# A planned eight-layer kernel: rotary rows swapped by DMA, and one group's keys and values made early

## The chip, the cores and the metric

The kernel runs on one NeuronCore of a Trainium2 chip. The metric is device time in microseconds (us) for one execution of the whole program. A core has five engines, each with its own instruction queue: TensorE (PE, matmuls, with PEld for its weight loads), VectorE (DVE), ScalarE (ACT), GpSimd (POOL) and SyncE (SP, which here only issues DMAs). Each engine takes its instructions in the order in which they stand.

## The reference

`x` is 64 sequences of 64 tokens with 128 features, `ctx` a context of the same size. Four layers follow each other, each with an attention and an FFN branch, gated and added to `x` after a layernorm:

```python
x = x + jnp.tanh(g_xattn[0]) * _L0_xattn_ref(_layernorm(x), ctx, ctx, ...)   # mLSTM
x = x + jnp.tanh(g_ffn[0]) * _L0_ffn_ref(_layernorm(x), ...)                 # mixture-of-experts attention
x = x + jnp.tanh(g_xattn[1]) * _L1_xattn_ref(_layernorm(x), ctx, lens, ...)  # 16 heads of 64, RMS-normed q and k
x = x + jnp.tanh(g_ffn[1]) * _L1_ffn_ref(_layernorm(x), ...)                 # one adapter of 8 per sequence
x = x + jnp.tanh(g_xattn[2]) * _L2_xattn_ref(_layernorm(x), ctx, ...)        # 16 heads of 8, rotary q and k
x = x + jnp.tanh(g_ffn[2]) * _L2_ffn_ref(_layernorm(x), ...)                 # top 2 of 8 experts of 176, one shared
x = x + jnp.tanh(g_xattn[3]) * _L3_xattn_ref(ctx, ctx, _layernorm(x), mask, ...)
x = x + jnp.tanh(g_ffn[3]) * _L3_ffn_ref(_layernorm(x), ...)                 # fake-quantised, one scale over all of x
```

Three of them matter here. In layer 1's attention the keys are `rms_norm(ctx @ Wk)` and the values `ctx @ Wv`: neither needs `x`. In layer 2's attention each head's features are rotated in pairs:

```python
xe, xo = x[..., ::2], x[..., 1::2]
re, ro = xe * cos - xo * sin, xe * sin + xo * cos
```

In layer 1's FFN every token gets `b_base` and its expert's `ba_up`.

## The kernel before

The 4096 tokens are 8 groups of 512 (4 tiles of 128). A unit of work is one layer of one group: a pair (n, g), where n from 0 to 7 counts the eight branches above. `ORDER` lists the 64 pairs; `program` walks it and lets each branch's function record its instructions. Nothing is issued then. `Plan` keeps each operation with what it depends on, and `Plan.order` afterwards puts them into queues: a list scheduler with a price per operation (`cost`), eight PSUM banks and a number of SBUF slots per size (`SLOTS`, 42 of 2 KB). An operation's rank is its place in the recording. An operation that opens a slot and depends on no other slot's content (a load, a memset) is tied to an earlier operation of its stream, so that it does not come too early; `behind` and `plan.after` add such ties by hand. While `plan.after` is set, each DMA that is recorded waits for that operation. Where the planner foresees PE idle for long enough it puts in filler matmuls of `ident` with itself (`keep_clock`; they carry line 2074), to keep TensorE's clock granted. On each engine the order so made is the order in which the chip runs.

The weights of branch n+1 are loaded on ACT's queue when the first group of branch n has been recorded (`weights[n + 1]`), with `plan.after` set to that group's first operation `begun[n]`; for the first branch this is done after its second group, and the two 2 MB expert tables `ve` and `oe` wait besides for marks in that group's gates.

The parts that the change touches:

- `l0_xattn`, the first branch: the gate values of a group go to DRAM and back twice (`gd`, `rd`) before the attention matmuls (L1021, L1029, L1045). `l0_ffn` has PE's largest groups, the value experts (L1208) and the output experts (L1263), which read the one-hot rows `ohd` by DMA (L1254); its values are moved to other partitions by SBUF-to-SBUF DMAs (L1224).
- `l1_xattn`: for a tile, `project` makes queries and keys (L1322 to L1333), then come the values (L1350), the transposes (L822, in `transpose4`) and their copies (L1364, L1366), and the scores.
- `l1_ffn`: the biases are added by a matmul of `pick`, the one-hot of the expert with a row of ones, with `W["bias"]` (L1557), both f32.
- `l2_xattn`: `rotated` makes the pair-swapped rows by a second matmul with a weight whose columns are swapped (`wqs`, `wks`, L1706), and multiplies both from PSUM by `cos` and `sin` on DVE (L1708, L1712).
- `l2_ffn`: 1584 hidden rows in 12 chunks of 128 and one of 48, for gate (L1834) and up (L1835); its down weights `wd` are loaded in 29 pieces (L1758) from ACT.

Weights are loaded by `load` (L739), the context by `ctx_T` (L813).

Of the kernel before, what the change touches and what calls it, by code (L numbers as in the profile page):

```python
# [27 lines left out]
P = 128  # L28
# [16 lines left out]
    "b2k": (2048, 42),  # L45
# [26 lines left out]
class View:  # L72
# [40 lines left out]
    def region(self, exact=False):  # L113
# [8 lines left out]
        key = (row, c0, v.shape[1:], v.strides[1:])  # L122
        if key in View.bits:
            return p0, p0 + v.shape[0], View.bits[key]
# [7 lines left out]
        return p0, p0 + v.shape[0], View.bits[key]  # L132

    def real(self):
# [9 lines left out]
        ap = [[step, self.v.shape[0]]] + [[st, n] for n, st in zip(self.v.shape[1:], self.v.strides[1:])]  # L144
# [74 lines left out]
def cost(op):  # L219
# [12 lines left out]
    if meth == "indirect_dma_start":  # L232
        return 1300.0, 2000.0, None
# [59 lines left out]
class Plan:  # L293
    def __init__(self, tc, slots):
# [6 lines left out]
        self.hold, self.urgent = [], False  # L301
# [16 lines left out]
    def add(self, eng, meth, args, kw):  # L318
# [65 lines left out]
        if op.opens and op.opens[0].pool is not None:  # L384
# [424 lines left out]
def ctx_T(k, g):  # L809

    t = k.tile([P, GT], tag="cT")
    with k.behind(*k.begun):
        k.nc.sync.dma_start(out=t, in_=k.a["ctxT"][:, g * GT : (g + 1) * GT])  # L813
    return t
# [282 lines left out]
def l0_ffn_weights(k):  # L1097
    k.l0f = {n: k.load("l0f_" + n) for n in ("wgate", "wq", "wk")}

    for n, m in (("ve", k.marks[4]), ("oe", k.marks[5])):  # L1100
        k.plan.after = m
        k.l0f[n] = k.load("l0f_" + n)
# [171 lines left out]
def l1_xattn_weights(k):  # L1274
    k.l1x = {n: k.load("l1x_" + n) for n in ("wq", "wk", "wv", "qn", "kn")}
# [7 lines left out]
    k.l1x["lens"] = k.load("l1x_lens", dt=I32)  # L1283


def l1_xattn(k):
# [51 lines left out]
    def unit(g, t, xT, cT, past):  # L1338
        tok = slice(t * P, (t + 1) * P)
        tt = g * TG + t  # L1340

        nq = [project(xT[:, tok], W["wq"], half, None) for half in range(2)]
        nk = [project(cT[:, tok], W["wk"], half, valid[:, tt : tt + 1]) for half in range(2)]

        vt = [k.tile([P, C, DH], tag="vt") for _ in range(2)]
        for b in range(2):
            pv = k.ps()
            k.plan.wait(nq[1], nk[1])
# [8 lines left out]
            nc.scalar.copy(vt[b].rearrange("p c d -> p (c d)"), pv)  # L1357

        qT, kT = [], []
        for half in range(2):  # L1360
            qT.append(k.tile([P, 4, P], tag="qT"))
            kT.append(k.tile([P, 4, P], tag="kT"))
            pq = transpose4(k, nq[half])
            nc.scalar.copy(qT[half].rearrange("p c i -> p (c i)"), pq)  # L1364
            pk = transpose4(k, nk[half])
            nc.scalar.activation(kT[half].rearrange("p c i -> p (c i)"), pk, AF.Copy, scale=wqk)  # L1366
# [67 lines left out]
    def whole(g):  # L1434
        xT, cT = ln_T(k, g), ctx_T(k, g)
# [8 lines left out]
        for t in range(TG):  # L1444
            unit(g, t, xT, cT, past)
# [755 lines left out]
```

## Time and profile before

| | us |
|---|---|
| median of 4 runs | 1994.06 (1988.18 to 2003.24) |
| profiled execution | 1999.16 |
| its span, first to last instruction | 1997.4 |
| PE busy in it | 1896.3 |
| of that, filler matmuls (L2074, 806 records) | 113.7 |
| DVE, ACT, POOL busy | 1358.5, 1031.5, 1012.2 |
| mean granted TensorE clock | 0.974 of full |

A row of the groups reads: line, engine, operation, output tile <- input tiles, shapes, count of records, busy time in us, mean of one in ns, idle time of the engine before them and what ended it. An f32 matmul stands in it as two records, a transpose or a bf16 matmul as one. Stretches are given in us from the span's start. In the chain of waits a piece is a start, a length and what ran. In the trace `b2k`, `b1k` and the like are SBUF slots by size, `ps` a PSUM bank.

### The profile page before, as it was taken

To read this page: it belongs to the slowest core of one execution; us is meant where nothing else is said; L and a number is where in the kernel's file an instruction comes from. 1 tells how busy PE (TensorE), PEld (TensorE's weight loads), DVE (VectorE), ACT (ScalarE), POOL (GpSimd) and SP (SyncE) were. 2 spreads that over 40 slices of the span, in tenths; PEclk is the share of its full clock that TensorE was granted. 3 is DMA by queue.
4 is the path that set the end of the run, shared out by engine and by line. 5 is a ranking of instruction groups with operands and counts; after the bars stand their busy time and mean duration, and the time that the engine had idled before them with its cause. 6 is when DMAs were issued, how large, how long until landed. Compare 5 with 4: busy or idle time off the path is not lost.

```text
span 1997.4 us, 45509 instructions
## 1 busy us (share of the span) xinstructions
PE 1896.3 (95%) x17127; PEld 1133.8 (57%) x17127; DVE 1358.5 (68%) x3172; ACT 1031.5 (52%) x2896; POOL 1012.2 (51%) x1656
## 2 busy tenths in 40 slices
PE   8999999989999999999999999999999999999997
PEld 6654457545545466746554466644555457774575
DVE  2667775767886577678775568676887376775468
ACT  5452277534445568835242577641436377444465
POOL 5621475424526667546214786433246774444745
PEclk8799999999999989999999999999999999999999
DMA  4223300142123200011133200014211400102311
GB/s 149 94 56 89 105 2 14 28 125 75 44 88 86 79 12 12 24 54 58 51 86 99 66 16 13 22 43 137 56 62 45 114 2 2 57 20 66 93 59 43
DMA packets 117836, 117.19 MB, mean 59 GB/s; under 512 B 56371, under 2 KB 76903, under 8 KB 117359
## 3 DMA queue, kind: packets, MB, share of 16 engines
q1 hardware_dynamic: 106680, 97.71, 17.7%
q10 hardware_dynamic: 7863, 10.23, 1.6%
q0 software_dynamic: 3072, 6.33, 1.1%
q8 instruction: 135, 2.21, 0.4%
q14 instruction: 86, 0.70, 0.1%
HBM read 98.53 MB, written 8.09 MB: 53 GB/s over the span
## 4 chain that ended last, share of the span: by engine, by line
PE 71%; DVE 10%; POOL 6%; DMA 4%; ACT 3%; issue 3%; SPq 1%; another core or an unknown queue 0%; ACTq 0%; DVEq 0%; POOLq 0%
PE ps L1208 10%; PE ps L1263 8%; PE ps L822 8%; PE ps L1840 4%; PE ps L1835 4%; PE ps L1834 4%; POOL b L760 4%; PE ps L1637 3%; PE ps L1428 3%; PE ps L2074 3%; PE ps L1322 3%; PE ps L1350 2%; PE ps L1415 2%; PE ps L1235 1%; PE ps L1599 1%
## 5 line engine op out<-in xcount | busy, mean ns | idle before, releaser
L760 POOL TENSOR_TENSOR b<-b,neghalf 128x8 f32<-128x8 f32 (+1 forms) x208 | 304.5, 1464 | 17.2
L1208 PE MATMUL ps<-w_l0f_ve,b2k 128*128 128x512 f32 x512 | 244.9, 617 | 11.5 <-DVE b2k L1432 5.7
L759 POOL TENSOR_SCALAR b<-b 128x8 f32<-128x8 f32 (+1 forms) x208 | 42.9, 206 | 379.9 <-DVE b L788 254.4
L1263 PE MATMUL ps<-b2k,w_l0f_oe 128*128 128x512 f32 x512 | 230.2, 598 | 5.0 <-DVE b2k L1261 5.0
L1214 DVE COPY_PREDICATED b2k<-b1k,ps 128x512 f32<-128x512 int32 x224 | 162.5, 726 | 64.6 <-PE ps L1208 41.8
L1261 DVE TENSOR_TENSOR b2k<-b2k,b2k 128x512 f32<-128x512 f32 x256 | 171.5, 723 | 31.1 <-DMA b2k<-ohd 13.1
L1081 DVE TENSOR_REDUCE b<-ps 128x8 f32<-128x512 f32 x224 | 146.0, 681 | 58.1 <-PE ps L1386 24.2
L1839 POOL TENSOR_TENSOR b2k<-b2k,b2k 128x512 f32<-128x512 f32 (+1 forms) x104 | 131.6, 1288 | 96.6 <-DMA b2k<-cwd 43.5
L1263 PEld LDWEIGHTS ps<-b2k,w_l0f_oe 128*128 128x128 f32 x512 | 94.8, 191 | 121.7 <-issue 83.0
L1208 PEld LDWEIGHTS ps<-w_l0f_ve,b2k 128*128 128x128 f32 x512 | 94.4, 196 | 111.4 <-issue 78.7
L1082 DVE TENSOR_TENSOR b4k<-ps,b 128x512 f32<-128x512 f32 x224 | 148.3, 677 | 8.0 <-PE ps L822 7.7
L822 PE MATMUL ps<-ident,b2k 128*128 128x128 f32 x896 | 132.5, 278 | 7.6 <-DVE b2k L1333 3.2
L822 PEld LDWEIGHTS ps<-ident,b2k 128*128 128x128 f32 x896 | 102.7, 141 | 63.1 <-issue 32.2
L822 PE MATMUL ps<-ident,b4k 128*128 128x128 f32 x896 | 129.4, 281 | 7.1 <-ACT b4k L1625 5.5
L1838 DVE TENSOR_TENSOR b2k<-b2k,ps 128x512 f32<-128x512 f32 (+1 forms) x104 | 70.6, 684 | 93.0 <-PE ps L1835 74.1
L1084 ACT ACTIVATE b4k<-b4k 128x64 f32<-128x64 f32 x512 | 125.4, 251 | 14.9 <-DVE b4k L1082 13.6
L822 PEld LDWEIGHTS ps<-ident,b4k 128*128 128x128 f32 x896 | 102.9, 143 | 52.2 <-issue 25.8
L1837 ACT ACTIVATE b2k<-ps 128x512 f32<-128x512 f32 (+1 forms) x104 | 61.2, 596 | 137.7 <-PE ps L1834 107.2
L2074 PE MATMUL ps<-ident 128*128 128x128 f32 x806 | 113.7, 295 | 4.6 <-issue 2.2
L1333 DVE TENSOR_TENSOR b2k<-ps,b 128x512 f32<-128x512 f32 x128 | 87.4, 685 | 44.7 <-POOL b L1330 26.2
L1327 DVE TENSOR_REDUCE b<-b2k 128x8 f32<-128x512 f32 x128 | 84.2, 677 | 42.1 <-ACT b2k L1324 41.5
L2074 PEld LDWEIGHTS ps<-ident 128*128 128x128 f32 x806 | 104.7, 206 | 13.1 <-issue 7.7
(366 smaller groups left out, 4108.0 us busy)
## 6 DMA issues: line engine op xcount, KB each, us to landing
b2k<-ohd SPq DMA_DIRECT2D x256, 128.0 KB
b2k<-cwd SPq DMA_DIRECT2D x40, 256.0 KB
b2k<-in_ctxT SPq DMA_DIRECT2D x32, 256.0 KB
b2k<-b2k SPq DMA_DIRECT2D x128, 64.0 KB
b2k<-cwd SPq DMA_DIRECT2D x16, 224.0 KB
b2k<-cwd SPq DMA_DIRECT2D x16, 192.0 KB
b2k<-cwd SPq DMA_DIRECT2D x16, 160.0 KB
b2k<-cwd SPq DMA_DIRECT2D x24, 96.0 KB
```

Source lines behind the costliest of these rows:

```text
L760: k.nc.gpsimd.tensor_tensor(out, out, k.neghalf[:, :n], ALU.pow)
L822: k.nc.tensor.transpose(ps[:, t * P : (t + 1) * P], src[:, t, :], k.ident)
L1081: nc.vector.tensor_reduce(mx, src, AX.X, ALU.max)
L1082: nc.vector.tensor_tensor(out, src, bc(mx, 2, S), ALU.subtract)
L1084: nc.scalar.activation(out[:, n, :], out[:, n, :], AF.Exp, accum_out=den[n])
L1208: nc.tensor.matmul(pe, xT[:, t * P : (t + 1) * P], W["ve"][:, e * 512 : (e + 1) * 512], start=True, stop=True)
L1214: nc.vector.copy_predicated(acc, bc(ohi[:, t * H : (t + 1) * H, e], 2, DH), pe.rearrange("p (h d) -> p h d", d=DH))
L1261: nc.vector.tensor_tensor(so, oT[c], pick[:, u, :], ALU.mult)
L1263: nc.tensor.matmul(py, W["oe"][:, n * P : (n + 1) * P], so, start=(n == 0), stop=(n == C * E - 1))
L1333: nc.vector.tensor_tensor(n.rearrange("p c (r d) -> p (c r) d", r=2), ps.rearrange("p (h d) -> p h d", d=DH), bc(r, 2, DH), ALU.mult)
L1839: nc.gpsimd.tensor_tensor(h[:cn], h[:cn], cb[:cn], ALU.mult)
L2074: plan.spare = (sys._getframe().f_lineno, k.ident, k.ident.t.writes[-1][0])
```

## The change

- `l2_xattn`'s `rotated` has one matmul. ACT adds the bias and copies the result to SBUF; two DMAs on SP write the swapped rows (even partitions from odd ones and the other way round) into a second tile; three SBUF operations multiply and add. For the keys the last two of them run on POOL.
- In `l1_xattn` the group that `ORDER` names first for this branch is `eager`: its context load, keys and values are recorded ahead of its layernorm, and without ties, so that they can run as early as their operands land. `wk`, `wv`, `qn`, `kn` and `lens` of this branch are loaded with layer 0's FFN weights, ahead of `ve` and `oe`. That context load is then the unit's first operation, and so `begun[2]`, which the loads of `l1_ffn_weights` wait for.
- `l1_ffn`'s bias is split into three bf16 parts that stand 32 rows apart and are summed by the matmul; `pick` is bf16.
- `l2_ffn`'s last chunk has one matmul for gate and up, with a weight `last` of 112 columns. Its weights are loaded in turn: gate, then up after a third of the unit recorded last, then down after two thirds, down on SP instead of ACT.
- The planner has 45 slots of 2 KB and another price for an indirect DMA; regions know strided partitions. `ORDER` is another.

```diff
-    "b2k": (2048, 42),
+    "b2k": (2048, 45),
...
     if meth == "indirect_dma_start":
-        return 1300.0, 2000.0, None
+        return 1220.0, 1700.0, None
...
-        if op.opens and op.opens[0].pool is not None:
+        if op.opens and op.opens[0].pool is not None and not self.eager:
...
 def l0_ffn_weights(k):
     k.l0f = {n: k.load("l0f_" + n) for n in ("wgate", "wq", "wk")}
 
+    k.l1x = {n: k.load("l1x_" + n) for n in ("wk", "qn", "kn", "wv")}
+    k.l1x["lens"] = k.load("l1x_lens", dt=I32)
+
     for n, m in (("ve", k.marks[4]), ("oe", k.marks[5])):
...
 def l1_xattn_weights(k):
-    k.l1x = {n: k.load("l1x_" + n) for n in ("wq", "wk", "wv", "qn", "kn")}
+    k.l1x["wq"] = k.load("l1x_wq")
...
     def whole(g):
-        xT, cT = ln_T(k, g), ctx_T(k, g)
+        early = [None] * TG
+        eager = g in k.eager
+        if eager:
+            cT = ctx_T(k, g, True)
+            for t in range(TG):
+                kT = [turned(n, wqk) for n in keys(g, t, cT)]
+                early[t] = kT, values(t, cT, kT)
+        xT = ln_T(k, g)
+        if not eager:
+            cT = ctx_T(k, g)
...
-            unit(g, t, xT, cT, past)
+            unit(g, t, xT, cT, past, early[t])
...
-    bias = k.l1f["bias"] = k.fixed("w_l1f_bias", [P, D])
-    nc.gpsimd.memset(bias, 0.0)
-    nc.scalar.dma_start(out=bias[:64], in_=k.a["l1f_bias"])
+    parts = k.l1f["bias"] = k.fixed("w_l1f_bias", [P, D], BF16)
...
+    for r in range(3):
+        nc.sync.dma_start(out=rest[32 * r : 32 * r + 8], in_=k.a["l1f_bias"][:8])
+        nc.sync.dma_start(out=rest[32 * r + 8 : 32 * r + 9], in_=k.a["l1f_bias"][32:33])
+    for r in range(3):
+        rows = slice(32 * r, 32 * r + 32)
+        nc.vector.tensor_copy(part, rest)
+        nc.vector.tensor_copy(parts[rows], part[rows])
+        nc.vector.tensor_tensor(rest, rest, part, ALU.subtract)
...
-        pick = k.tile([P, NB, S], tag="pick")
-        nc.vector.tensor_scalar(pick, bc(owns, 2, S), k.ident[:, 32:33], None, ALU.add)
+        pick = k.tile([P, NB, S], BF16, tag="pick")
+        nc.vector.tensor_scalar(pick, bc(owns, 2, S), k.l1at[:, 8:9], None, ALU.add)
...
     def rotated(src, weight, bias, last):
 
-        out = []
-        for s, table in (("", "cos"), ("s", "sin")):
-            ps = k.ps()
-            nc.tensor.matmul(ps, W[weight + s], src, start=True, stop=True)
-            o = k.tile([P, NB, S], tag="rot" + s)
-            nc.vector.scalar_tensor_tensor(
-                o, ps.rearrange("p (b s) -> p b s", s=S), W[bias + s], bc(W[table], 1, NB), ALU.add, ALU.mult
+        ps = k.ps()
+        nc.tensor.matmul(ps, W[weight], src, start=True, stop=True)
+        y, ys = (k.tile([P, GT], tag="rot") for _ in range(2))
+        nc.scalar.activation(y, ps, AF.Identity, bias=W[bias])
+        for r in range(2):
+            nc.sync.dma_start(
+                out=ys.rearrange("(i r) n -> r i n", r=2)[r], in_=y.rearrange("(i r) n -> r i n", r=2)[1 - r]
             )
-            out.append(o)
-        last.tensor_tensor(out[0], out[0], out[1], ALU.add)
-        return out[0].rearrange("p b s -> p (b s)")
+        yv, ysv = (v.rearrange("p (b s) -> p b s", s=S) for v in (y, ys))
+        nc.vector.tensor_tensor(yv, yv, bc(W["cos"], 1, NB), ALU.mult)
+        last.tensor_tensor(ysv, ysv, bc(W["sin"], 1, NB), ALU.mult)
+        last.tensor_tensor(y, y, ys, ALU.add)
+        return y
...
 def l2_ffn_weights(k):
-    k.l2f = {n: k.load("l2f_" + n) for n in ("gate", "wg", "wu")}
+    k.l2f = {"gate": k.load("l2f_gate")}
+
+    last = k.l2f["last"] = k.fixed("w_l2f_last", [P, 112])
+    k.nc.gpsimd.memset(last, 0.0)
+    at, end = k.done
+    for n, name in enumerate(("wg", "wu")):
+        t = k.l2f[name] = k.fixed("w_l2f_" + name, [P, 1536])
+        k.nc.scalar.dma_start(out=t, in_=k.a["l2f_" + name][:, :1536])
+        k.nc.scalar.dma_start(out=last[:, 64 * n : 64 * n + 48], in_=k.a["l2f_" + name][:, 1536:])
+        k.plan.after = k.plan.ops[at + (end - at) * (n + 1) // 3]
...
-            k.nc.scalar.dma_start(
+            k.nc.sync.dma_start(
...
-            pg, pu = k.ps(), k.ps()
-            nc.tensor.matmul(pg[:cn], W["wg"][:, c0 : c0 + cn], xT, start=True, stop=True)
-            nc.tensor.matmul(pu[:cn], W["wu"][:, c0 : c0 + cn], xT, start=True, stop=True)
+            pg = k.ps()
+            if cn < P:
+                pu = pg[64 : 64 + cn]
+                nc.tensor.matmul(pg[: 64 + cn], W["last"], xT, start=True, stop=True)
+            else:
...
-        "02 00 03 01 10 11 20 21 30 40 31 12 05 13 41 04 50 51 60 61 22 70 23 32 33 71 06 07 42 15 43 14 "
-        "53 52 25 63 62 24 72 35 34 16 17 45 44 55 73 54 26 27 36 37 65 64 75 74 46 47 56 57 66 67 76 77"
+        "03 00 02 01 10 11 20 21 30 31 13 12 40 41 05 04 50 51 60 61 23 22 70 71 33 43 32 42 15 14 06 07 "
+        "53 52 63 62 25 24 35 45 34 44 16 17 73 72 55 54 65 26 64 27 36 46 37 47 75 56 74 57 66 67 76 77"
...
+        k.eager = [g for n, g in ORDER if n == 2][:1]
...
+            k.done = at, len(plan.ops)
```

What moved in `l1_xattn` keeps its operations. `keys` is the two key projections, `values` the four matmuls and two copies of the values, and `turned` four transposes and the copy behind them:

```python
def turned(n, scale):
    out = k.tile([P, 4, P], tag="nT")
    flat = out.rearrange("p c i -> p (c i)")
    if scale is None:
        nc.scalar.copy(flat, transpose4(k, n))
    else:
        nc.scalar.activation(flat, transpose4(k, n), AF.Copy, scale=scale)
    return out
```

## The prediction

> **What bounds the kernel now.** I read the page's busy shares first, then the stretches of 50 us, then the filler matmuls alone in the same stretches, then the groups by shape, and last the chain of waits. The page:
>
> ```profile
> span 1997.4 us, 45509 instructions
> ...
> PE 1896.3 (95%) x17127; PEld 1133.8 (57%) x17127; DVE 1358.5 (68%) x3172; ACT 1031.5 (52%) x2896; POOL 1012.2 (51%) x1656
> ```
>
> PE bounds it: 1896.3 of 1997.4 us busy, 101.1 us idle; no other engine is above 68%. The stretches (columns: sum length, then busy time and count of PE, PEld, DVE, ACT, POOL, granted clock, DMA share, GB/s) show where the 101.1 us lie:
>
> ```profile
> 0.00:50.00 50.00, 42.62 (x268) 30.30 (x270) 14.22 (x63) 25.54 (x55) 29.16 (x105) 0.90 0.46 150
> 50.00:100.00 50.00, 49.88 (x446) 33.92 (x443) 32.03 (x146) 22.61 (x60) 31.52 (x62) 0.80 0.29 93
> ...
> 400.00:450.00 50.00, 42.52 (x288) 22.16 (x287) 34.09 (x69) 19.45 (x45) 14.36 (x27) 0.93 0.45 126
> ```
>
> The same view for L2074 alone (PE, PEld, clock, DMA) shows how much of PE's work is filler, the dummy matmuls that the planner puts where it foresees PE idle:
>
> ```profile
> 0.00:50.00 50.00, 21.07 (x142) 20.02 (x142) 0.90 0.46 150
> 50.00:100.00 50.00, 11.59 (x72) 10.06 (x72) 0.80 0.29 93
> ...
> sum 2000.00, PE 113.71 PEld 104.70; mean PE 2.84 PEld 2.62
> ```
>
> So 113.7 us is filler: 32.7 in the first 100 us, 0.8 until 1650, the rest, 80.2, after 1650. The kernel has three parts: a head of 100 us that waits on latencies, a middle of 1550 us that is pure PE throughput, and a tail of 350 us that again waits. In stretches of 10 us the head shows its second cost:
>
> ```profile
> 40.00:50.00 10.00, 8.75 (x68) 5.70 (x70) 3.92 (x13) 3.85 (x10) 6.79 (x17) 0.65 0.39 116
> 50.00:60.00 10.00, 10.00 (x92) 6.23 (x90) 5.73 (x27) 4.50 (x10) 0.92 (x3) 0.50 0.43 164
> 60.00:70.00 10.00, 10.00 (x69) 7.22 (x66) 5.01 (x24) 5.22 (x17) 6.43 (x12) 0.50 0.23 61
> ```
>
> PE is busy all the time at half the clock. Shapes and their times:
>
> ```profile
> L2074 PE MATMUL ps<-ident 128*128 128x128 f32 x806 | 113.7, 295 | 4.6 <-issue 2.2 <-POOL ident L841 1.4 <-DVE b2k L1708 0.6
> ...
> L1557 PE MATMUL ps<-w_l1f_bias,b2k 128*128 128x128 f32 x64 | 13.2, 290 | 0.0
> ...
> L1834 PE MATMUL ps<-b2k,w_l2f_wg 128*48 128x512 f32 x16 | 8.4, 606 | 0.0
> ...
> L1706 PE MATMUL ps<-b2k,w_l2x_wqs 128*128 128x512 f32 x16 | 8.4, 605 | 0.0
> ...
> L1835 PE MATMUL ps<-b2k,w_l2f_wu 128*48 128x512 f32 x16 | 8.2, 594 | 0.0
> L1706 PE MATMUL ps<-b2k,w_l2x_wks 128*128 128x512 f32 x16 | 8.2, 592 | 0.0
> ```
>
> An f32 matmul has two records, so x16 is 8 matmuls. Their pace is in the chain (start, length, what):
>
> ```profile
> 99.72 3.44 PE ps L1208 x8
> ...
> 192.87 3.98 DMA b2k<-b2k
> ...
> 325.45 1.87 PE ps L1350 x8
> ...
> 343.04 1.90 PE ps L822 x16
> ...
> 414.78 9.21 DMA b2k<-ohd
> ...
> 437.69 3.81 DMA w_l2f_wd<-in_l2f_wd
> ...
> 1345.61 2.49 DMA b2k<-b2k
> ...
> 1933.89 3.35 PE ps L2074 x30
> ```
>
> A 512-column matmul takes 3.44/4 = 0.86 us, a values matmul 1.87/4 = 0.47, a transpose 1.90/16 = 0.12, a filler 3.35/15 = 0.223 (0.282 averaged over the run, 113.7/403).
>
> **The change, part by part.**
>
> *PE work removed.* The built program has 16 rotation matmuls less (weights wqs, wks): 16 x 0.86 = 13.8. The last chunk's two 48-column matmuls become one of 112 columns: 8 x 0.86 = 6.9. The 32 bias matmuls become bf16. No row has that operation in bf16; the bounds are nothing gained (0; a loss is excluded, since a bf16 matmul leaves one record where f32 leaves two) and all of it (32 x 0.223 = 7.1). The nearest row, L2041's bf16 128x128, busy 8.3 us for 64, is 0.13 each against 13.2/32 = 0.41 in the L1557 row: 0.69 saved, so 32 x 0.223 x 0.69 = 4.9. Sum 25.6.
>
> *Keys and values moved (`keys`, `values`, `turned`).* One group, four tiles: 8 x 0.86 + 16 x 0.47 + 32 x 0.12 = 18.2 us of PE, plus 8 each of ACT squares, kT copies and vt copies (0.60, 0.69, 0.59: 15.0), 8 DVE reductions and multiplications (0.68 + 0.69: 11.0), 8 POOL scalings, powers and masks (0.20 + 1.65 + 0.28: 17.0). They leave the middle, where PE is the bound, for the head, where POOL is busy 60.7 of 100 us, ACT 48.2, DVE 46.3.
>
> *Fillers.* The built program has 456 instead of 403: 57 instead of 107 ahead of the first value experts, 398 instead of 293 in the tail. In the head 50 x 0.305 (32.7/107) = 15.3 less; in the tail 105 x 0.223 to 0.282 = 23.4 to 29.6 more. So the tail takes back most of what the middle gains: it waits on the latencies of the last groups' layers, and these do not get shorter.
>
> *Sum of PE's stream:* -25.6 - 15.3 + 26.5 = -14.4 (-19.7 to -6.4 by the bounds); the moved 18.2 us cancel, their gain is in the fillers. The new ORDER, the three more b2k slots, the planner's new price of an indirect DMA and the strided regions issue nothing themselves; what they do to the order is in these counts and in what follows.
>
> *Idle time that the plan does not foresee.* (a) From 400 to 450 PE loses 7.5 us idle and, at a clock of 0.93, 3.5 more. There ACT issues 29 pieces of l2f_wd (418.5 to 441.5, median 336 ns) just behind two 792 KB loads, and the pick rows take 9.21 us to land. The change puts them on SP and spreads the three weights over the unit before. Between 0 and -11.0; I take -5: the same 2.4 MB still have to land, and SP now has 29 x 0.34 = 9.9 us of issues, with the rd write and reads of a layer-0 group queued behind them, which are what can be late next. (b) The head. Ten more DMA issues stand on ACT there (0.44 us each, as the l1x_qn and l1x_kn issues at 76 us took: 4.4 us), five ahead of ACT's first normalisation; layer 1's FFN loads and row-table writes now hang on `begun[2]`, which has become the early ctxT load, so they come here too, and on SP they stand between the gates' writes and reads. Unit 2's gate matmuls are queued on PE behind key matmuls that wait for a 512 KB load. Bounds: -13.5 (full clock from 40 to 70 us, where 0.65, 0.50 and 0.50 were granted: 3.5 + 5 + 5; full-array work now stands there) and +18.2 + 4.4 = 22.6 (all moved PE work done at half clock, and the issues exposed). I take +3, nearer the issue rows than either end. (c) The swaps. Each of 16 calls replaces one matmul by an ACT pass (0.69) and two 128 KB SBUF moves (issue 0.61 each, as L1224's; landing 2.49 to 3.98 in the chain), with 32 issues, 19.6 us, more on SP, where pick rows and value moves queue behind them. Hidden they cost 0 - the 128 moves of L1224 kept PE waiting 3.0 us in all - and exposed 16 x 3.98 = 64. The middle has other groups' work to cover them; in the tail the last four calls are partly in the fillers. I take +2. DVE stays equal (two PSUM passes of 0.74 and a sum become three SBUF passes of 0.69 to 0.72), POOL gains 8 x 1.27 = 10.2 us, two more table loads cost ACT 2.6: and the three-part split of the bias adds 11 small DVE operations and seven small loads once: all under PE, nothing; without that cover the ACT passes (16 x 0.69) and POOL's would be 21 us.
>
> Together -14.4 - 5 + 3 + 2 = -14.4. The profiled execution took 1999.16 us (1997.4 span, 1.8 around it), 5.1 above the median of 1994.06; taken off the median, 1979.7, say 1980, which is 0.7% down.
>
> On (b), the row says PE was busy 10.00 of 10 us in two stretches in a row and still granted 0.50. The Trainium skill, "TensorE: Matmul & The Clock Gate", "Part 1: The HAM clock gate", says that about 3.4 us of sustained activity release the throttle; by that the moved work would run at full clock and (b) would be the issues alone, +4.4, and the sum -13.0. By the row, were it to hold for the moved work, it would be +22.6 and +5.2. [...] On (c), "DMA: Bandwidth & Descriptors", section "Bandwidth", advises batches of 1 MiB or more, which speaks against paying two 128 KB moves for 0.86 us of PE; by the fit in its "Anatomy of one DMA" (for moves that GpSimd issues), 2.0 us and bytes over 436 KB per us, a move is an estimated 2.3 us, and 16 exposed would be 37 us instead of the 64 by our rows.
>
> **The rivals.** (1) My forecast, 1974 to 1987: stream shorter, idle unchanged. (2) Swaps and SP queue exposed: at 16 calls x 0.9 us, a quarter of a landing, the sum is -14.4 - 2 + 14.4 = -2, 1992: same. For it: SP serves in order, and L1224 stood 265.9 us behind POOL's scaling there. Against it: those 3.0 us. (3) Slower: the head. If PE's in-order queue stalls on the key weights, the gates of units 2 to 4 come late and PE stays cold with the moved work in it: +22.6 instead of +3, and the 512 KB load 5 us late besides (a 256 KB one took 5.21 us at the start): -14.4 + 19.6 + 5 = +10, 2004. It decides from a head 24 us longer than forecast. Against it: unit 1's gates stand ahead of the keys. (4) Better: the head warms early (-13.5 for +3) and the jam at 400 goes (-11 for -5): -14.4 - 16.5 - 6 = -37, 1957. (5) That it does nothing: excluded by the counts of the built program.
>
> **How the numbers follow.** A measurement of this kernel tells 0.5%, 10 us, from no change. Chances: (1) 0.45, most of it beyond 10 us; (2) 0.26; (3) 0.14; (4) 0.15. Faster: 0.15 + 0.39 of (1) + 0.02 of (2) = 0.56; slower 0.13 of (3); same 0.31. The range leaves out half of (4)'s far end and of (3)'s: 1960 to 2004.
>
> **What would show it.** The L1706 groups with wqs and wks gone, 16 records less on the 48-column shapes, the bias group near 4 us; PE busy near 1882 with fillers near 125; the first L1208 work (its new line) near 100 us; no chain pieces of l2f_wd on ACT near 430; PE idle still near 100. Wrong if the clock in the first 100 us falls under 0.8, if the swapped tile appears among PE's releasers with more than 10 us, or if PE idle grows by more than 10 us.

## The result, and the profile after

| | before | after |
|---|---|---|
| median, us | 1994.57 (69 runs, 1986.97 to 2003.24) | 1994.58 (44 runs, 1983.03 to 2015.5) |
| profiled execution, its span | 1999.16, 1997.4 | 2001.22, 1999.5 |

The ratio is 0.9998, with a 95% interval of 0.9987 to 1.001: no change, where 0.7% faster was forecast. The page of the changed kernel, its span and its engines' busy times:

```profile
span 1999.5 us, 45609 instructions
...
PE 1890.5 (95%) x17153; PEld 1136.7 (57%) x17153; DVE 1365.1 (68%) x3175; ACT 1047.0 (52%) x2914; POOL 1041.9 (52%) x1666
```

PE's busy time fell by 5.8 us, not by the 14 forecast, and its idle time rose from 101.1 to 109.0. The groups by shape show that the work itself went as described:

```profile
L2135 PE MATMUL ps<-ident 128*128 128x128 f32 x912 | 123.8, 288 | 2.5 <-POOL ident L845 1.4 <-issue 1.1
...
L1747 PE MATMUL ps<-b2k,w_l2x_wq 128*128 128x512 f32 x16 | 8.6, 618 | 0.0
L1747 PE MATMUL ps<-b2k,w_l2x_wk 128*128 128x512 f32 x16 | 8.4, 606 | 0.0
L1890 PE MATMUL ps<-b2k,w_l2f_last 128*112 128x512 f32 x16 | 8.2, 592 | 0.0
...
L1600 PE MATMUL ps<-w_l1f_bias,b1k 128*128 128x128 bf16 x32 | 7.4, 231 | 0.0
```

The groups with wqs and wks are gone, one group of 112 columns stands for two of 48, the bias costs 7.4 us instead of 13.2 (near 4 was expected), and the fillers (now L2135) take 123.8 instead of 113.7. The stretches of 50 us, with the same columns as in the prediction, first of the kernel before, where the prediction does not show them:

```profile
500.00:550.00 50.00, 48.80 (x416) 25.82 (x414) 42.64 (x103) 24.32 (x110) 28.03 (x53) 1.00 0.17 44
700.00:750.00 50.00, 46.06 (x708) 31.27 (x705) 35.28 (x83) 32.84 (x98) 32.82 (x67) 0.90 0.04 12
1750.00:1800.00 50.00, 46.50 (x608) 37.31 (x607) 37.77 (x97) 25.22 (x57) 21.65 (x59) 0.94 0.06 18
```

And of the changed kernel:

```profile
0.00:50.00 50.00, 39.93 (x222) 23.81 (x222) 24.03 (x83) 31.68 (x66) 39.49 (x110) 0.91 0.57 183
50.00:100.00 50.00, 49.07 (x348) 28.08 (x349) 27.22 (x115) 23.28 (x55) 29.09 (x59) 0.75 0.27 77
...
400.00:450.00 50.00, 43.85 (x260) 24.43 (x260) 33.90 (x80) 11.92 (x32) 19.15 (x30) 0.90 0.49 139
450.00:500.00 50.00, 50.00 (x398) 25.84 (x397) 31.74 (x67) 19.57 (x93) 17.08 (x33) 1.00 0.14 33
500.00:550.00 50.00, 41.49 (x247) 19.44 (x246) 39.89 (x72) 21.31 (x48) 22.29 (x24) 0.90 0.39 125
...
700.00:750.00 50.00, 46.82 (x724) 33.99 (x725) 30.48 (x79) 31.73 (x92) 25.36 (x55) 0.86 0.04 11
...
1750.00:1800.00 50.00, 46.72 (x436) 35.41 (x437) 26.97 (x91) 21.25 (x45) 18.83 (x39) 0.86 0.06 20
```

The hole from 400 to 450 is still there, at a lower clock (0.90 for 0.93), and there is a second one from 500 to 550, where the kernel before had PE busy for 48.80 us at full clock. From 700 to 750 and from 1750 to 1800 PE is busy for about as long as it was, but colder (0.86 for 0.90 and 0.94). In stretches of 10 us the head of this profile is as cold as it was:

```profile
40.00:50.00 10.00, 3.83 (x48) 2.19 (x48) 3.31 (x13) 7.64 (x19) 8.98 (x20) 0.70 1.00 371
50.00:60.00 10.00, 9.32 (x40) 4.71 (x40) 3.34 (x14) 1.28 (x3) 2.17 (x4) 0.50 0.49 157
60.00:70.00 10.00, 10.00 (x90) 7.03 (x88) 4.57 (x20) 4.31 (x15) 4.17 (x7) 0.50 0.36 85
```

From 40 to 50 us the DMA engines are busy all the time (share 1.00, 371 GB/s, where 116 were moved before) and PE stands for 6.2 us. The chain of waits has these pieces where it had L1208's matmuls, `ohd` and `l2f_wd` before (start, length, what):

```profile
111.91 3.65 PE ps L1215 x8
...
410.80 9.03 DMA b2k<-b2k
...
521.23 3.92 DMA w_l2f_wu<-in_l2f_wu
526.77 2.91 DMA b2k<-ohd
```

And PE's waits (line, releaser: us in all, times, the longest). First the kernel before:

```profile
PE ps L1263 <- DVE b2k L1261: 5.0, 6, 2.4
PE ps L1235 <- DMA b2k<-b2k: 3.0, 4, 1.2
PE ps L1021 <- DMA b2k<-rd: 2.9, 1, 2.9
```

Then the same three in the changed kernel:

```profile
PE ps L1270 <- DVE b2k L1268: 11.4, 10, 6.6
PE ps L1242 <- DMA b2k<-b2k: 7.1, 3, 6.2
...
PE ps L1025 <- DMA b2k<-rd: 6.5, 2, 4.8
```

The two longest single waits, 6.6 and 6.2 us, are the holes: the output experts (L1270) behind the product with the picked rows (L1268), and the scores of layer 0's FFN (L1242) behind the moves of its values.

**A balance.** From the trace's PE records, its clock records and the fillers' line, PE's span splits into four terms: real work at full clock; fillers at full clock; the surcharge for cold time, half of PE's busy time while the granted clock was a half; and idle. It was made for the profiles on record and for a second pair, taken on one chip (`r_before`, `r_after` below). Where two matmuls overlap, the time is counted to the earlier one.

| us | before | after | | r_before | r_after | | forecast |
|---|---|---|---|---|---|---|---|
| real work | 1751.4 | 1717.9 | -33.5 | 1750.7 | 1718.7 | -32.0 | -25.6 |
| fillers | 97.8 | 109.6 | +11.8 | 97.0 | 110.2 | +13.2 | +11.2 |
| cold surcharge | 47.1 | 62.9 | +15.8 | 46.6 | 49.8 | +3.2 | 0, with idle |
| idle | 101.2 | 109.1 | +7.9 | 95.4 | 108.1 | +12.7 | |
| span | 1997.4 | 1999.5 | +2 | 1989.8 | 1986.8 | -3 | -14.4 |

So more PE work went than forecast, the fillers took back what was forecast, and 16 to 24 us came back as cold clock and idle, of which nothing was forecast in sum. Split where the prediction splits the kernel, at 100 and 1650 us, the two terms lie here:

| us | before | after | r_before | r_after |
|---|---|---|---|---|
| cold surcharge, head | 15.4 | 14.3 | 15.4 | 5.4 |
| middle | 23.5 | 37.4 | 19.7 | 32.3 |
| tail | 8.2 | 11.2 | 11.5 | 12.2 |
| idle, head | 7.5 | 11.0 | 7.7 | 12.5 |
| middle | 62.5 | 61.7 | 59.1 | 59.5 |
| tail | 31.2 | 36.3 | 28.6 | 36.2 |

In the middle PE does not stand longer, but it runs cold for longer: 12.6 to 13.9 us more surcharge. The idle time grew in the head and in the tail.

One profile is a sample of one, but every run has its granted clock. The clock that was not granted, (1 - clock) x span, averaged over all runs but one slow one (the kernel before beside `x_after`, 2362.89 us), is:

| | before | after |
|---|---|---|
| beside `r_after` | 53.4 (23 runs) | 69.6 (12 runs) |
| beside `x_after` | 37.9 (22 runs) | 51.4 (12 runs) |

That is 13.5 to 16.2 us more in the changed kernel, on two chips independently. Without it the medians would stand 16.5 and 12.1 us apart (1993.53 to 1993.19 and 1955.9 to 1957.3, less these terms), and the forecast's 14.4 is between the two. But that is a sum and not a cause: this loss also counts time in which PE stands idle at half clock, and one control below (`c_before_price`) has 18.6 us more of it than the kernel before and takes the same time.

### The profile page after: what moved, and what is told of

Read it like the earlier page. It is cut to its first block, busy times and chain, and to the rows that moved or that the text cites. A ratio compares the mean times of both kernels' runs of the same rounds, so it can differ in the third digit from the quotient of the medians.

```text
span 1999.5 us, 45609 instructions
## 1 busy us (share of the span) xinstructions
PE 1890.5 (95%) x17153; PEld 1136.7 (57%) x17153; DVE 1365.1 (68%) x3175; ACT 1047.0 (52%) x2914; POOL 1041.9 (52%) x1666
## 4 chain that ended last, share of the span: by engine, by line
PE 70%; DVE 11%; POOL 6%; DMA 6%; issue 4%; ACT 3%; SPq 1%; another core or an unknown queue 0%; DVEq 0%; ACTq 0%; POOLq 0%
PE ps L1215 10%; PE ps L826 8%; PE ps L1270 7%; PE ps L1328 4%; PE ps L1899 3%; PE ps L1893 3%; PE ps L2135 3%; PE ps L1894 3%; PE ps L1449 3%; POOL b L762 3%; PE ps L1680 3%; DVE b2k L1268 2%; PE ps L1365 2%; PE ps L1242 2%; DMA b2k<-cwd 2%
## 5 line engine op out<-in xcount | busy, mean ns | idle before, releaser
L1270 PE MATMUL ps<-b2k,w_l0f_oe 128*128 128x512 f32 x512 | 237.0, 607 | 12.3 <-DVE b2k L1268 11.4
L1215 PE MATMUL ps<-w_l0f_ve,b2k 128*128 128x512 f32 x512 | 240.9, 608 | 1.1 <-DVE b L790 0.8
L1268 DVE TENSOR_TENSOR b2k<-b2k,b2k 128x512 f32<-128x512 f32 x256 | 179.8, 748 | 51.0 <-DMA b2k<-ohd 19.9
L1270 PEld LDWEIGHTS ps<-b2k,w_l0f_oe 128*128 128x128 f32 x512 | 95.5, 193 | 131.9 <-issue 81.8
L1224 POOL TENSOR_TENSOR b2k<-b2k,b 128x512 f32<-128x512 f32 x32 | 34.0, 1062 | 180.6 <-DVE b2k L1221 105.2
L2135 PE MATMUL ps<-ident 128*128 128x128 f32 x912 | 123.8, 288 | 2.5 <-POOL ident L845 1.4
L2135 PEld LDWEIGHTS ps<-ident 128*128 128x128 f32 x912 | 114.8, 200 | 12.4 <-issue 8.5
L1419 POOL TENSOR_TENSOR b4k<-b4k,b 128x512 f32<-128x512 f32 x64 | 66.6, 1060 | 101.5 <-DVE b L1416 50.1
```

Of the source, the lines that this page charges most:

```text
L1215: nc.tensor.matmul(pe, xT[:, t * P : (t + 1) * P], W["ve"][:, e * 512 : (e + 1) * 512], start=True, stop=True)
L1268: nc.vector.tensor_tensor(so, oT[c], pick[:, u, :], ALU.mult)
L1270: nc.tensor.matmul(py, W["oe"][:, n * P : (n + 1) * P], so, start=(n == 0), stop=(n == C * E - 1))
L2135: plan.spare = (sys._getframe().f_lineno, k.ident, k.ident.t.writes[-1][0])
```

## The experiments

The runs were taken in five sets, each on one chip with the kernel before beside it. On some chips the kernel before takes 1994 to 1999 us and on others 1956 to 1959, so only ratios to the kernel before of the same set are used.

**Each part undone (first set).** The edits, in short:

```diff
 e1_rot_matmul: -  y = ps + bias; two DMAs y -> ys; y*cos + ys*sin
                +  two matmuls (W["wq"], W["wqs"]), times cos and sin from PSUM
 e2_no_eager:   -  k.eager = [g for n, g in ORDER if n == 2][:1]
                +  k.eager = []            (l1x loads back in l1_xattn_weights)
 e3_wd_on_act:  -  k.plan.after = k.plan.ops[at + (end - at) * (n + 1) // 3]
                -  k.nc.sync.dma_start(out=wd[...
                +  k.nc.scalar.dma_start(out=wd[...
 e4_pe_only:    the kernel before, + bias in three bf16 parts, + "last" of 112 columns
```

> The changed kernel with the rotation made by the second matmul again (weights wqs and wks back, no swap by DMA; 44 b2k slots instead of 45, because the weights take 1 KB). The profiles of before and after give this balance of the 2.1 us by which the profiled spans differ: PE's real work at full clock 1751.4 to 1717.9 (-33.5), fillers about +12, PE busy at half clock 94.1 to 125.9 us (+15.9 lost), PE idle 101.2 to 109.1 (+7.9). Theory S: the swaps and the 32 issues on SP make the waits behind the colder clock and the idle. Then this kernel has PE busy at half clock back near 94 and idle near 101, while it pays 13.8 us of matmuls: 1994.6 - 16 - 8 + 14 = 1985 or less. Theory N: the swaps are innocent; then 13.8 us of matmuls come back, the plan has 495 fillers for 456 (39 x 0.22 = 8.7 more), and it takes 2005 to 2017. Between them, 1990 to 2000: the swap is worth about what it costs.

> The changed kernel without the early keys and values: all groups make them in their own unit, the four l1x weights load with the layer's others, and layer 1's FFN loads hang on the first layer-1 attention unit again. The plan has 555 fillers instead of 456, 121 of them in the head instead of 57. If the early work does what the prediction said (18.2 us of PE in the place of fillers): 99 fillers x 0.22 to 0.28 = 22 to 28 us slower, 2010 to 2022. If the head pays it back (cold PE, loads that come early and collide): within 5 us of 1994.6.

> The changed kernel with l2f_wd's 29 pieces on ACT's queue again and the three weights not spread over the unit before; all else as changed (459 fillers for 456). If the loads on SP are what holds the value moves back at 414 us (6.15 us of PE idle) and the pick rows at 524 us (6.63): both gaps go, with the clock they cost, and this takes 1980 to 1988. If spreading them helped, as the prediction said (-5): 1996 to 2005. If neither: 1992 to 1997.

> The kernel before with only the two edits that take PE work away and add no wait: the bias matmuls in bf16 with the bias in three parts, and the last chunk's two 48-column matmuls as one. Order, slots, loads' queues and the rotation stay. 6.9 + 4.9 = 11.8 us of PE less by the prediction (0 to 7.1 for the bias), 435 fillers instead of 403 (+7 us). If PE's stream sets the time: 1985 to 1992. If what is taken from PE turns into waits wherever it was: 1993 to 1997.

Ratios to the kernel before: e1 1.0186 (1.0156 to 1.0216), e2 1.0086 (1.0063 to 1.0109), e3 1.0096 (1.0067 to 1.0125), e4 1.0053 (1.0031 to 1.0075). The expectations were in microseconds from 1994.6, but the kernel before took 1958.6 here, and the changed kernel was not in this set. All four are slower than the kernel before and, as the later sets show, than the changed kernel. Even e4 is, which has PE work taken away and no wait added; its order is another, with 435 fillers for 403. Its real work at full clock is 1743.8 us, 7 to 8 less than in the two profiles of the kernel before (1751.4 and 1750.7) for 11.8 forecast, and its mean loss by the clock is 51.6 us where the kernel before beside it has 38.7. That e3 would be the faster kernel is excluded; why it is slower is not told by it.

**The kernels again, and two controls (second set).** The controls only set the planner's price of an indirect DMA, so that the same instructions come in another order, with other fillers (420 for 403 and 502 for 456):

```diff
 c_before_price (the kernel before):
-        return 1300.0, 2000.0, None
+        return 1220.0, 1700.0, None
 e7_price (the changed kernel): the reverse
```

> The changed kernel itself, again, beside the kernel before. In the last call the kernel before took 1958.6 us where it had taken 1994.57, and all four kernels stood 0.5 to 1.9% above it, also the one that only takes PE work away. If the ratio of the two kernels is a property of the programs, 0.9998 comes back (0.997 to 1.003). If it hangs on how long DMA and waits take where they run, the changed kernel, with 16 x 2 swaps and more waits, gains less than the kernel before from whatever made that one 36 us faster: a ratio of 1.005 to 1.015.

> The kernel before itself, for its profile in the same surroundings as the other three. If it takes 1994 us, its balance is the known one (PE idle 101.2, PE busy at half clock 94.1, real work at full clock 1751.4, fillers 105.5). If it takes 1959: 36 us have to come out of these terms; by the profile of the kernel with only PE work taken away (idle 68.9, half clock 79.0) about 30 of them out of idle, and 8 out of the clock.

> A control: the kernel before, all instructions as they were, but for the planner's price of an indirect DMA (1220 and 1700 ns instead of 1300 and 2000, as in the changed kernel). It only moves the order (420 fillers instead of 403, all 17 more in the tail). Theory P, that any new plan moves the time by several us whatever the work: 4 to 15 us away from the kernel before, either way. Theory W, that the work and its waits set the time: within 4 us (17 fillers x 0.22).

> The mirror control: the changed kernel with the old price of an indirect DMA (1300 and 2000 ns). Its instructions are the changed kernel's, in another order, with 502 fillers for 456 (46 more, in the tail: 10 us if they lie on the path). Theory P: 4 to 15 us away from the changed kernel, either way. Theory W: 0 to 10 us slower by the fillers, and the same idle and half-clock time.

r_after took 1.0000 (0.9973 to 1.0026) of the kernel before, so the first result stands; r_before took 1991.5 us. c_before_price took 0.9995 (0.9982 to 1.0008), e7_price 1.0067 (1.005 to 1.0084). Theory W holds for c_before_price and theory P for e7, but the balance of c_before_price says more than its time. The mean clock of the profiled execution, first of r_before, then of c_before_price:

```profile
core 0: 1989.8 us, clock 0.974
```

```profile
core 0: 1989.8 us, clock 0.964
```

The span is the same and the clock is not. Its terms against r_before are real work -4.7, fillers +2.9, idle -10.5, cold surcharge +12.4. With the same real instructions the terms trade against each other and the time stays. The other control costs 0.7%: against r_after its profile has +10.8 of real work, +8.4 of fillers, -0.4 of idle and -4.6 of cold surcharge. So a new order with its fillers can move the time by as much as the change was forecast to bring, and the first set's undone parts can't be read as the parts' prices: each of them was planned anew.

**The same beside the changed kernel, and the order of units (third set).**

```diff
 e5_after_order_b (the changed kernel):
-        "03 00 02 01 10 11 20 21 30 31 13 12 40 41 05 04 ...
+        "02 00 03 01 10 11 20 21 30 40 31 12 05 13 41 04 ...
```

> The changed kernel, as the control of this call: the first call's four kernels had only the kernel before beside them, and there that one took 1958.6 us instead of 1994. 1.000 (0.997 to 1.003) of the kernel before if that one takes about 1994 us again; if it takes about 1959 again, 1.005 to 1.015, as argued for the second call.

> The changed kernel with the rotation by a second matmul again and 44 b2k slots, now beside the changed kernel. 13.8 us of matmuls come back and 39 fillers (8.7 us). Theory N, swaps are hidden: 1.005 to 1.011 of the changed kernel. Theory S, the swaps cost about what they save: 0.996 to 1.004. A gain beyond that (under 0.996) would say that the swaps are what ate the change.

> The changed kernel without the early keys and values, now beside the changed kernel. In the second call the changed kernel's head had 4.8 us more idle than the kernel before (12.5 against 7.7) and its first 1650 us 12.5 more. If the early work is worth its 99 fillers (22 to 28 us): 1.011 to 1.014 of the changed kernel. If the head and the loads that come early with it pay it back: 0.997 to 1.003. If they cost more than they bring: under 0.997; the first call, where this kernel took 0.991 of the one with matmul rotation, points to the last two.

> The changed kernel with the ORDER of units of the kernel before; all else as changed, 429 fillers for 456 (27 x 0.22 = 6 us less). The changed kernel's waits that push PE to half clock stand at fixed places in both its profiles (413, 524, 711, 894, 955, 1344, 1703 and 1749 us). Theory O, the new order set them there: most go, PE busy at half clock falls from 100 to 126 us to 80 or less, 0.985 to 0.994 of the changed kernel. Theory W, they come with the swaps, the loads on SP and the early work: other places, the same sum, 0.995 to 1.000 by the fillers.

x_after took 1.0013 (0.9987 to 1.0038): no difference here either, though the kernel before took 1956 us. x1 took 1.0144 (1.0114 to 1.0175), x2 1.0094 (1.0065 to 1.0123), e5 1.0023 (1.0002 to 1.0044). That x1 is 1.3% above the changed kernel excludes theory S in the form that undoing the swaps wins time; its profile has 1747.4 us of real work, 30.1 more than x_after, where 13.8 were expected for the matmuls, so how much of the 1.3% is the swap and how much the new order is not separated. x2, 0.8% above, lies below the price of its 99 fillers and above nothing, with the same reservation. e5 is the most telling. The pages of x_after and then of e5:

```profile
span 1943.4 us, 45609 instructions
...
PE 1856.8 (96%) x17153; PEld 1117.1 (57%) x17153; DVE 1362.9 (70%) x3175; ACT 1046.6 (54%) x2914; POOL 1043.7 (54%) x1666
```

```profile
span 1961.2 us, 45547 instructions
...
PE 1879.1 (96%) x17099; PEld 1130.3 (58%) x17099; DVE 1364.1 (70%) x3175; ACT 1050.7 (54%) x2915; POOL 1034.8 (53%) x1666
```

Both have 16241 records of real matmuls, and e5 has 27 fillers less; yet its PE is busy for 22.3 us more. At full clock the real work is 1717.3 us in x_after and 1738.5 in e5: the order decides how PE's work packs. So with the kernel before's order of units the change takes only 12 to 13 us off the real work (1751.4 and 1750.7 before). And the mean loss by the clock over all runs is 51.4 us in x_after and 39.9 in e5 (37.9 in the kernel before). The new order thus brings shorter busy time and a colder clock together, and the time differs by 3.4 us. Theory O was right on the mean loss and wrong on the time; the two profiles do not show the loss (58.1 us of PE's busy time at half clock in x_after, the fastest of its 12 runs, and 74.5 in e5). The two holes of the changed kernel are not in e5, whose longest wait for the picked product is 2.1 us and for the value moves 0.4:

```profile
400.00:450.00 50.00, 48.71 (x506) 26.76 (x504) 45.11 (x99) 32.76 (x94) 23.01 (x40) 1.00 0.47 132
500.00:550.00 50.00, 48.62 (x256) 24.49 (x255) 39.35 (x75) 19.58 (x46) 23.84 (x28) 1.00 0.37 110
```

**One cause at a time in a fixed order (fourth set).** To keep the order, these kernels plan exactly as the changed kernel does, and alter the list of operations only as it is issued:

```diff
-        result = self.order()
+        result = tweak(self.order())
 f1_rot_twice:    the matmuls of L1747 issued twice
 f2_swap_on_act:  the DMAs of L1751: o.eng = "scalar"
 f3_l2f_early:    the DMAs of L1803, L1804, L1812 moved to where the plan's time is 290 us
 f5_rows_later:   the DMAs of L1513, L1516, L1517 moved to 110 us
```

> The changed kernel in its own order, instruction for instruction, but each of the 16 rotation matmuls is issued twice, the second over the first: 13.8 us more PE work (16 x 0.86) in the middle and tail, no new wait. The changed kernel stands at 1.000, 1.000 and 1.001 of the kernel before. Theory T, PE's stream sets the time: +13.8 us, 1.007 of the kernel before. Theory V, PE time taken out or put in is made up by waits: less than half of it, 1.003 or lower. This says what a microsecond of removed PE work was worth.

> The changed kernel in its own order, but the 32 swap DMAs are issued by ACT, right behind ACT's own copy in its order, instead of by SP. In the changed kernel's profile SP stands 125.5 us behind ACT for them (61.5 + 48.2 + 15.8), with pick rows and value moves queued behind. Theory c, that is where part of the new idle comes from: SP's waits at that line go, PE idle and half-clock time fall, 0.990 to 0.997 of the kernel before. Rival: SP has the time, and ACT pays 32 issues of 0.6 us (19.6 us): 1.000 to 1.006.

> The changed kernel in its own order, but the loads of l2f_wg, l2f_wu, their last columns and the 29 pieces of l2f_wd are all issued near 300 us, where DMA moves 7 GB/s, instead of from 366 to 500 us in the plan's time. In the changed kernel PE waits 3.7 to 6.2 us for value moves near 410 us and 6.6 to 6.9 for a pick product near 515 to 524, with 17 to 20 us at half clock behind them. Theory a, these come of the loads: both gaps shrink to under 2.5 us and 8 to 18 us go: 0.991 to 0.996 of the kernel before. Rival, the gaps have another cause (the order, SP's waits): gaps stay, 0.998 to 1.002.

> The changed kernel in its own order, but the 10 writes of layer 1's row table, which hang on the early ctxT load and so stand on SP between the gates' writes and reads in the first 60 us, are issued from 110 us of the plan's time on. In the changed kernel PE idles 10.6 to 12.5 us in the first 100 us against 7.5 to 7.7 before; the rd reads make 6.5 to 7.6 of it against 2.9. Theory b: the rd wait falls back to about 3 and 3 to 8 us go, 0.996 to 0.9985 of the kernel before. Rival, the early keys ahead of the gates on PE make that wait: no change, 0.999 to 1.002.

f1 took 1.0033 (1.0011 to 1.0055), f2 0.9993 (0.9971 to 1.0014), f3 0.9991 (0.997 to 1.0012), f5 1.0004 (0.9986 to 1.0022). The changed kernel was not in this set nor in the next; its three ratios average 1.0004, so f2, f3 and f5 stay within 0.13% of it. Two of them nevertheless did at their place what was expected. PE's wait for the picked product in x_after and then in f2:

```profile
PE ps L1270 <- DVE b2k L1268: 13.1, 10, 6.9
```

```profile
PE ps L1270 <- DVE b2k L1268: 7.1, 10, 2.9
```

And two stretches, in x_after and then in f3 (two chips, on both of which the kernel before takes 1956 us):

```profile
400.00:450.00 50.00, 48.64 (x243) 24.39 (x244) 32.88 (x69) 10.40 (x49) 24.03 (x47) 0.94 0.39 109
...
500.00:550.00 50.00, 40.10 (x358) 22.45 (x357) 39.99 (x85) 27.19 (x57) 18.83 (x34) 0.93 0.25 78
```

```profile
400.00:450.00 50.00, 48.80 (x305) 26.71 (x302) 42.16 (x96) 16.50 (x47) 24.28 (x39) 1.00 0.50 134
...
500.00:550.00 50.00, 43.86 (x284) 21.28 (x283) 45.16 (x83) 24.44 (x55) 30.50 (x39) 1.00 0.30 96
```

With the loads moved, both stretches run at full clock, though PE is still idle for 6.1 us of the second. The longest wait for the value moves is 0.5 us in f3, where the seven profiles of this order with the loads in place have 3.2 to 6.6, so the late loads did hold the moves back. The longest wait for the picks is 1.9 us in f3 and 2.9 in f2, for 4.2 to 6.9 in the six that have neither edit. But f3 has a new gap of 4.1 us at 335 us, f2 one of 2.5 at 511, and the end does not come noticeably sooner. The chain of r_after shows how the swaps and the loads meet at that place:

```profile
510.42 1.67 POOL b2k L1757
...
512.13 4.05 DMA w_l2f_wu<-in_l2f_wu
...
517.30 0.44 SPq L1261
...
517.80 3.01 DMA b2k<-ohd
```

The sum of a rotation on POOL, the landing of l2f_wu, a pick-row issue on SP and its landing stand one behind the other in it; PE's wait there is 6.9 us.

f5's longest wait for the rd rows is 3.8 us, where the eight other profiles of this order have 4.8 to 6.3 and the two of the kernel before 2.9 and 3.0. So the row table's writes are one part of that wait, as far as one profile tells, and here too the time stays where it is.

**Two causes together, and a second dose (fifth set).** f6_both has the edits of f2 and f3; f7_rot_thrice issues the matmuls of L1747 three times.

> The changed kernel in its own order with both edits: the 32 swap DMAs issued by ACT, and the l2f weights loaded near 300 us. Alone they took 0.9993 and 0.9991 of the kernel before, and the gaps near 410 and 515 us shrank in the one to 3.2 and 2.9, in the other under 2. Theory M, the two hide each other, since either leaves one of the waits at that place: together 0.992 to 0.996. Theory V, waits take turns and idle elsewhere makes it up: 0.997 to 1.000.

> The changed kernel in its own order with each of the 16 rotation matmuls issued three times: 27.6 us more PE work. Theory T, PE's stream sets the time: 1.014 to 1.015 of the kernel before. Theory V, with the slope of the first dose (about 0.4): 1.005 to 1.008. A bend, the first 13.8 us absorbed by idle and the next paid in full: 1.009 to 1.011.

f6 took 0.9988 (0.997 to 1.0006) and f7 1.0051 (1.0025 to 1.0077). Both speak for theory V. In f6 the wait for the value moves is short again (0.7 us at the longest), but the one for the picks is back, so its fall in f2 and f3 does not hold with both edits:

```profile
PE ps L1270 <- DVE b2k L1268: 10.1, 8, 5.3
```

The pages of f6 and then of f7:

```profile
span 1991.4 us, 45572 instructions
...
PE 1880.0 (94%) x17151; PEld 1129.5 (57%) x17153; DVE 1366.1 (69%) x3175; ACT 1045.9 (53%) x2914; POOL 1042.1 (52%) x1666
```

```profile
span 1998.4 us, 45733 instructions
...
PE 1898.6 (95%) x17215; PEld 1137.6 (57%) x17217; DVE 1365.7 (68%) x3175; ACT 1047.2 (52%) x2914; POOL 1039.5 (52%) x1666
```

f7 against f6: real work at full clock +29.8 us, cold surcharge -12.3, idle -11.6, fillers +1.2: span +7. f6 has two other edits, and f7's profile is the fastest of its seven runs; against r_after, of another chip but with f7's loads and swaps, the terms are +29.5, -9.5, -8.3 and +0.1. That is the change's balance of work, cold and idle time with the sign turned. f1's profile does not show it (idle -1.4, cold +8.8 against x_after, whose profile is the fastest of its runs). Over all runs the clock's loss is 61.9 us in f7 and 68.0 in f6. Against the changed kernel's 1.0004, the first dose cost 0.0029 x 1956 = 5.7 us of 13.8 (0.41 of its length), the second 0.0047 x 1999 = 9.4 of 27.6 (0.34). By f7's interval the slope is between 0.15 and 0.53: a microsecond of PE work put in at these places (12 of the 16 matmuls stand in the middle, 4 in the tail) costs an estimated 0.3 to 0.4 of itself. One for one is excluded.

## Why the prediction was wrong

- *What bounds the kernel.* "A middle of 1550 us that is pure PE throughput" is the step that carries the error, and with it the term of nothing for cold and idle time below. PE was busy for 95% of the span, but by the doses PE time there is worth 0.3 to 0.4 of its length. In f7's profile PE's idle and cold time is smaller with the added work. That the same price holds for work taken away, and for the bias and last-chunk matmuls as for the rotations, is argued from the balance and not shown by a run of its own; e4, which only takes PE work away, has another order too and is slower. Nor does it make the whole miss: PE's stream got 18.8 to 21.7 us shorter, which at 0.34 to 0.41 is an estimated 6 to 9 us (3 at the slope's lower bound), and the result allows at most 2.6.
- *PE work removed*: forecast -25.6, measured -32.0 to -33.5. The bias gave 5.8 (13.2 to 7.4) for 4.9, and two groups of 48 columns (16.6) became one of 8.2. The rest lies within what a new order does to PE's packing (21 us between x_after and e5). Right in kind; that the size is near is partly luck, since with the ORDER of the kernel before the same parts took off 12 to 13 us.
- *Keys and values moved; fillers*: head -11.4 (27.8 to 16.4) for -15.3, tail +23.4 (69.4 to 92.8) for +23.4 to +29.6. Right: as PE's busy time, in which the forecast counts, the head's fillers fell by 14.8 (32.7 to 17.9). That the tail takes back most of what the middle gains was right too.
- *Idle that the plan does not foresee, (a) the jam, -5*: wrong. It stayed at 400 to 450 and got a twin at 500 to 550. f3 shows that in this order the l2f loads delay the value moves and, less surely (f6), the picks: loads do jam here, as the mechanism said, but spreading them over the unit put them beside these. The order has a part in it, since e5 spreads the same loads by the same rule and has neither hole.
- *(b) the head, +3*: right in size in the pair on record (idle +3.5, cold surcharge -1.1), not in the other (+4.8 and -10.0, in sum -5.2). The loads that come early do delay the rd rows, in part, as far as f5's one profile tells.
- *(c) the swaps, +2*: not contradicted, and not measured apart. On SP they were blamed with some reason, since f2 shortens the longest pick wait by 4 us, but all 32 moved off SP are worth 0.11% of the changed kernel, with an interval from 0.33% faster to 0.10% slower. POOL paid 24.5 us for the swapped product and the sum (1.68 and 1.38 each), where the sum alone had cost 10.2 before: 14.3 more for 10.2 forecast. PE waited 0.6 us for it.
- *The sum of (a) to (c), 0.* This is the term that failed: cold surcharge and idle measured +23.7 and +15.9. I priced the clock at two places only, the jam and the head, and charged the middle at full clock. In the profile after, the four waits of 2.2 to 6.6 us between 410 and 960 us are followed by 6.8 to 13.7 us at half clock, part of it still idle: with 2.5 to 6.2 us of cold surcharge each costs more than its length. The new ORDER was said to "issue nothing" and was priced by its fillers alone, while e5 shows 11.5 us of mean clock loss with it, against 21 us of better packing.
- *The bound for being wrong.* "PE idle grows by more than 10 us" came true in the second pair (+12.7) and nearly in the first (+7.9). The clock in the first 100 us did not fall under 0.8 (0.91 and 0.75), and the swapped tile does not stand among PE's releasers with more than 10 us (0.6).
- *The rivals.* The time of rival (2), 1992, came true, but f2 does not show its mechanism. The Trainium skill, "TensorE: Matmul & The Clock Gate", "Part 1: The HAM clock gate", cited for (b), would have the moved work at full clock after about 3.4 us of sustained activity. The profile after has 0.50 from 50 to 70 us with 9.32 and 10.00 of 10 us busy, as the row had it; r_after has 1.00 from 60 to 70 us with 9.86 busy. Neither end of (b) is what came. Nor does work of full height ensure it: r_before has 0.50 from 1708 to 1724 us, where PE is busy for 15.5 of 16 us with matmuls of 128 rows.

What stays open: why the clock loss of the same instructions can differ by 18.6 us with the order (53.4 in the kernel before, 72.0 in c_before_price, over all their runs), which chain through the other engines keeps the time where it is while PE's terms trade, and so what ate the part of the shorter stream that the doses do not explain.

## What to carry to other kernels

A PE that is 95% busy need not be the bound: issue some of its matmuls twice in an unchanged order, and the slope hints at what a microsecond removed can bring before any is removed. Where a planner orders everything, an undone part is another order, worth up to 0.7% here with no instruction but the fillers changed; compare in a fixed order, by altering only what is issued. And set the granted clock beside busy and idle time: PE's work went down here and its cold clock up, which the busy share counts as work.

## What the runs showed of the hardware

The scatter of one program's runs goes mostly with the clock. Over the 46 runs of the changed kernel that have a clock, the time and the mean granted clock have a correlation of -0.93, and taking (1 - clock) x span off each run's time brings the standard deviation from 7.5 to 3.1 us.

The same program took 1993 us on one chip and 1957 on another. In the two profiles (spans 1986.8 and 1943.4) the real work, 1718.7 and 1717.3 us, and the fillers, 110.2 and 110.4, agree; idle (108.1 and 86.6) and the cold surcharge (49.8 and 29.1) make the difference. What makes the waits shorter there was not tried.
